# Moving a layer's input loads from ScalarE's queue to SyncE's, behind a small store

## The chip, the cores and the metric

The kernel runs on one core of one Trainium2 chip. The core has five engines that run their own instruction streams side by side: TensorE (PE in the profile; its weight loads are shown as PEld), VectorE (DVE), ScalarE (ACT), GpSimd (POOL) and SyncE (SP). A load or store is a DMA: one engine issues it, and the transfer then runs beside the engines. The issues of an engine stand in its program like its other instructions and are taken in order; the profile shows them as ACTq or SPq.

The metric is the time of one execution in microseconds (us), as the median of several runs.

## The reference

Four layers run one after the other on x, which is 4 sequences of 1024 tokens with 256 channels:

```python
x = x + _L0_attn_a_ref(_layernorm(x), W_in, b_in, params_log, W_mid, ...)   # linear recurrence
x = x + _L0_ffn_ref(_layernorm(x), ...)                                     # top-32 gated product
x = x + _L0_attn_b_ref(_layernorm(x), Wq, Wkv_down, Wk_up, Wv_up, Wo)       # attention, 8 heads
x = x + _L0_ffn_ref(_layernorm(x), ...)                                     # the same ffn again
```

The change lies in the first layer. Cut to what matters, it is:

```python
u = jnp.einsum('btd,edh->ebth', x, W_in) + b_in          # three products: in_r, in_i, o
lam = jnp.exp(jax.lax.complex(-nu, theta))
uc = jax.lax.complex(gamma * in_r, gamma * in_i)
_, h = jax.lax.associative_scan(combine, (f, uc), axis=1)   # h[t] = lam * h[t-1] + uc[t]
out2 = jnp.einsum('ebtd,edh->ebth', jnp.stack([h.real, h.imag]), W_mid) + b_mid
out = out2[0] - out2[1] + o
y = jax.nn.gelu(out @ w1_w + w1_b, approximate=False)
y = y @ w2_w + w2_b + out
y = (y - mean) * rsqrt(var + LN_EPS) * ln_g + ln_b
```

## The kernel before

The 4096 tokens are eight blocks of 512 (`NBLK` is 8). A block holds every second token of one sequence, so two blocks make a sequence, and the recurrence runs over pairs of tokens. Each block of x is a tile of 128 partitions by 4 by 256 values, 512 KB, and stays in on-chip memory through all four layers. `load_x(engine, blk)` (L1040) loads one block on the queue of the engine that is named.

The first layer is class `Lru`:

- Its constructor issues the weights' loads on ScalarE (L217, L223, L225) and splits the input weights into two parts each (L219 on ScalarE, L220 on POOL).
- `head(xs)` (L357) normalizes one block. VectorE takes statistics of four tiles (L133, L134) and forms the reciprocal roots in a chain of small steps (L55 to L66, L136). ScalarE applies them (L145), PE transposes (L147), and the transposed block is split into a cast (L160, ScalarE) and a difference (L161, VectorE), called xnt. The first such cast is remembered as `xnt_first`.
- `tables` and `first_weights` (L230, L277) make tables of cosines and sines (L269 to L275) and turned weights (L354, L355) on VectorE and ScalarE.
- `states(xnts, c)` (L381) makes the products into the "pu" banks (L170), evacuates them on ScalarE (L390) and runs the recurrence on VectorE (L402 to L416; L410 is the scan). Each evacuation is appended to `evacuated`; one call appends two.
- `outputs` (L422) makes, for one block, the products into the "po" banks (L170 and L437), evacuates them on ScalarE into ot (L438), multiplies by w1 (L443, "pu" banks), applies the gelu (L446), multiplies by w2 (L452, "po" banks again), adds on VectorE (L455), transposes back (L465), and normalizes; POOL multiplies by the gain and adds the base of `brow` (L482, L483) and adds the result to x (L484).

There are two banks each of "pu", "po", "py" and "pt". A block's outputs use the two "po" banks twice, and L455 is what frees them the second time.

`ffn_weights` (L984) loads and prepares what the second layer needs: `lint` (four loads, L1010), `wf` (L1011), and three rows, which go through a buffer `v` of one copy. For each row POOL clears v (L1017), three loads of 1 KB fill three of its partitions (L1019), and ScalarE and POOL turn it into a sum of three bf16 parts (L1020 to L1025; the results are linb twice and bias). The next row cannot be loaded before the last step on the one before is done.

The order in which each engine takes its instructions is fixed when the program is built: a scheduler simulates the program in time (`schedule_with_timeline_sim=True`, L1303), fills each engine with what is ready, and prefers what stands earlier in the text. `tc.issue_after(ins)` puts what the block under it holds behind `ins` in the order of one engine, the engine of `ins`; it is an order, not a wait for `ins` to end, and work that the block holds on other engines is not bound by it.

In the kernel before the loads stand as follows: blocks 0 and 1 on SP at the very start; the weights on ScalarE; blocks 2 and 3 on ScalarE behind `xnt_first`; `brow` on ScalarE behind the fourth evacuation; blocks 4 to 7 and all of `ffn_weights` on ScalarE behind the eighth evacuation, which is the last one of the second sequence.

Of the kernel before, what the change touches and what calls it, by code (L numbers as in the profile page):

```python
# [10 lines left out]
F32 = mybir.dt.float32  # L11
# [10 lines left out]
P = 128  # L22
B = 4
T = 1024
D = 256
# [3 lines left out]
NBLK = B * T // 512  # L29
# [143 lines left out]
def by_block(v):  # L173

    return [
        v[b * T : (b + 1) * T, :].rearrange("(q p r) d -> r p q d", p=P, r=CH)[r] for b in range(B) for r in range(CH)
    ]
# [796 lines left out]
def run(*gens):  # L974
    for g in gens:
        for _ in g:
            pass
# [6 lines left out]
def ffn_weights(nc, rp, cp, w, lint, lin_t, w_ffn, rows):  # L984
    vecs = w.vecs


    grp = cp.tile([P, 32], F32, tag="grp", name="grp")
    nc.gpsimd.memset(grp, 1.0)
    nc.gpsimd.affine_select(  # L990
        out=grp, in_=grp, compare_op=ALU.is_ge, fill=0.0, base=0, pattern=[[-4, 32]], channel_multiplier=1
    )
    nc.gpsimd.affine_select(
        out=grp, in_=grp, compare_op=ALU.is_ge, fill=0.0, base=3, pattern=[[4, 32]], channel_multiplier=-1
    )
    for s in range(2):
        for k in range(KD):
            nc.gpsimd.tensor_scalar(
                w.cw[:, k, s * 32 : (s + 1) * 32],
                grp,  # L1000
                vecs[:, V_CW + 2 * s + k : V_CW + 2 * s + k + 1],
                0.0,
                ALU.mult,
                ALU.add,
            )
    nc.gpsimd.memset(lint, 0.0)
    for s in range(2):
        for k in range(KD):
            r = k * 64 + s * 32
            nc.scalar.dma_start(lint[r : r + 32, s, :], lin_t[s, k * 32 : (k + 1) * 32, :])  # L1010
    nc.scalar.dma_start(w.wf, w_ffn)  # L1011

    nc.gpsimd.memset(w.ones, 1.0)
    parts = [slice(32 * i, 32 * i + 32) for i in range(3)]
    for dst, at in ((w.linb[:, 0:D], 0), (w.linb[:, D : 2 * D], D), (w.bias, 4 * D)):
        v = rp.tile([P, D], F32, tag="v", name="v")
        nc.gpsimd.memset(v, 0.0)  # L1017
        for i in range(3):
            nc.scalar.dma_start(v[32 * i : 32 * i + 1, :], rows[0:1, at : at + D])  # L1019
        nc.scalar.copy(dst, v)  # L1020
        nc.gpsimd.tensor_tensor(v, v, dst, ALU.subtract)
        for i in (1, 2):
            nc.scalar.copy(dst[parts[i], :], v[parts[i], :])
        nc.gpsimd.tensor_tensor(v[parts[2], :], v[parts[2], :], dst[parts[2], :], ALU.subtract)
        nc.scalar.copy(dst[parts[2], :], v[parts[2], :])  # L1025
# [3 lines left out]
def tile_kernel(ctx: ExitStack, tc: tile.TileContext, x_in, w_lru, vecs_in, rows, w_ffn, lin_t, w_attn, w_down, out):  # L1029
    nc = tc.nc  # L1030
# [9 lines left out]
    def load_x(engine, blk):  # L1040
        engine.dma_start(blocks[blk], by_block(x_in)[blk])
# [9 lines left out]
    w = Weights()  # L1051
    w.ident, w.vecs = ident, vecs
    w.wf = cp.tile([P, KD, D], F32, tag="wf", name="wf")
    lint = cp.tile([P, 2, D], F32, tag="lint", name="lint")
# [5 lines left out]
    f1 = Ffn("f1", tc, bp, x, w)  # L1060
# [3 lines left out]
    with ExitStack() as c1:  # L1064
        psum = Banks(c1.enter_context(tc.tile_pool(name="ps1", space=PSUM)), {"pu": 2, "po": 2, "py": 2, "pt": 2})

        brow = c1.enter_context(tc.tile_pool(name="brow", bufs=1)).tile([P, 2, D], F32, tag="brow", name="brow")
        lru = Lru(tc, c1, ident, vecs, brow, w_lru, psum)
        xb = [x[4 * k : 4 * k + 4] for k in range(NBLK)]
        xnt = [lru.head(xb[0])]  # L1070
        lru.tables(lambda: xnt.append(lru.head(xb[1])))
        with tc.issue_after(lru.xnt_first):
            for blk in range(2, 4):
                load_x(nc.scalar, blk)
        h = [[lru.states(xnt, c) for c in range(KD)]]
        lru.output_weights()
        with tc.issue_after(lru.evacuated[3]):
            nc.scalar.dma_start(brow.rearrange("p a b -> p (a b)"), rows[0, 2 * D : 4 * D].partition_broadcast(P))
        xnt += [lru.head(xb[k]) for k in (2, 3)]
        h.append([lru.states(xnt[2:4], c) for c in range(KD)])  # L1080
        for k in range(NBLK):
            last = k >= NBLK - 2
            if k == 0:
                with tc.issue_after(lru.evacuated[7]):
                    for blk in range(4, NBLK):
                        load_x(nc.scalar, blk)
                    ffn_weights(
                        nc, c1.enter_context(tc.tile_pool(name="rows", bufs=1)), cp, w, lint, lin_t, w_ffn, rows
                    )
            if k < NBLK - 1:  # L1090
                run(lru.outputs(k % CH, xb[k], xnt[k], h[k // CH], (0, 1), last))

            b = k // CH + 1
            if 2 <= b < B:
                if k % CH == 0:
                    h.append([])
                h[b].append(lru.states(xnt[b * CH : (b + 1) * CH], k % CH))
            if k + 4 < NBLK:
                xnt.append(lru.head(xb[k + 4]))
            if 2 <= k < NBLK - 2:  # L1100
                run(f1.head(k - 2, lru.sp, psum, "pt"))
        for blk in range(4, NBLK - 3):
            run(f1.head(blk, lru.sp, psum, "pt"))
        k = NBLK - 1
        ot, zt = lru.buffers()
        halves = [
            lru.outputs(k % CH, xb[k], xnt[k], h[k // CH], (i,), last, tag, [v[:, :, c : c + 256] for v in (ot, zt)])
            for i, tag, c in ((0, "pu", 0), (1, "po", 256))
        ]
        for i in (0, 0, 1):  # L1110
            next(halves[i])
        run(f1.head(NBLK - 3, lru.sp, psum, "pt"))
        for i in (0, 1, 0, 1, 0, 1, 1):
            next(halves[i])
        with tc.issue_after(lru.last_gelu):
            run(f1.head(NBLK - 2, lru.sp, psum, "pt"))
        run(*(f1.head(NBLK - 1, lru.sp, psum, "pu", (i,), "lx", "zt") for i in range(2)))

    with ExitStack() as c2:
# [7 lines left out]
        at = Attention(tc, x, ident, ident64, wqk, wvo, wd, sp, wp)  # L1127
        with ExitStack() as c4:
# [14 lines left out]
            first = at.prepare(0, 0, psum, "at")  # L1143
# [163 lines left out]
```

## Time and profile before

| what | us |
|---|---|
| median of three runs | 1532.92 |
| lowest and highest run | 1526.67, 1534.85 |
| the profiled execution | 1534.08 |
| its span, first to last instruction | 1532.4 |
| busy PE, DVE, ACT, POOL in the span | 1295.5, 1183.2, 1017.3, 681.6 |
| mean granted PE clock | 0.937 |
| issue of blocks 2 and 3 on ACTq | 15.79 and 16.23 |
| issue of brow on ACTq | 46.01 |
| issue of blocks 4 to 7 on ACTq | from 73.17 |
| first store of the first layer on SPq (L527) | 135.45 |

The first layer lasts until about 295 us, when SP begins to load for the second. A row of the timeline reads: start, length, engine, line, operation, output from inputs, shapes, how many; in brackets how long the engine had stood idle just before and what ended that. A row of the waits reads: who waited for whom, the total, how often, the longest. A row of the windows gives each engine's busy time in that stretch with the number of its instructions, then the clock that PE was granted (1.00 is full), the share of the DMA engines' time, and GB/s.

### The profile page before, as it was taken

To read this page: it belongs to the slowest core of one execution; us is meant where nothing else is said; L and a number is where in the kernel's file an instruction comes from. 1 tells how busy PE (TensorE), PEld (TensorE's weight loads), DVE (VectorE), ACT (ScalarE), POOL (GpSimd) and SP (SyncE) were. 2 spreads that over 40 slices of the span, in tenths; PEclk is the share of its full clock that TensorE was granted. 3 is DMA by queue.
4 is the path that set the end of the run, shared out by engine and by line. 5 is a ranking of instruction groups with operands and counts; after the bars stand their busy time and mean duration, and the time that the engine had idled before them with its cause. 6 is when DMAs were issued, how large, how long until landed. Compare 5 with 4: busy or idle time off the path is not lost. (4 is left out here: it accounts for less than half of the span.)

```text
span 1532.4 us, 28699 instructions
## 1 busy us (share of the span) xinstructions
PE 1295.5 (85%) x10136; PEld 960.3 (63%) x10136; DVE 1183.2 (77%) x3674; ACT 1017.3 (66%) x2148; POOL 681.6 (44%) x849
## 2 busy tenths in 40 slices
PE   5879998697898898888988989899999998666775
PEld 3635455376676766766766767677777776434454
DVE  8976665697878887878778687776676675499998
ACT  5353433466887877797778687877776776476664
POOL 2033332162545454544544543445443534067876
PEclk9989999699999999999999999999999999679888
DMA  3010000321454334434433335334445454000000
GB/s 117 26 47 15 19 23 21 123 94 56 76 98 89 64 76 74 73 74 80 84 73 69 68 72 87 62 71 84 70 75 92 73 95 83 1 15 24 22 25 28
DMA packets 288609, 96.51 MB, mean 63 GB/s; under 512 B 268233, under 2 KB 284626, under 8 KB 288466
## 3 DMA queue, kind: packets, MB, share of 16 engines
q1 hardware_dynamic: 283024, 88.50, 28.5%
q10 hardware_dynamic: 5442, 6.18, 1.2%
q8 instruction: 80, 1.31, 0.3%
q14 instruction: 63, 0.52, 0.1%
HBM read 16.01 MB, written 11.53 MB: 18 GB/s over the span
## 5 line engine op out<-in xcount | busy, mean ns | idle before, releaser
L893 POOL TENSOR_TENSOR pd<-pr,pd 128x1024 f16<-128x1024 f32 x128 | 273.3, 2141 | 247.5 <-ACT pd L892 183.2
L885 DVE TENSOR_REDUCE nm<-sc 128x1 f32<-128x1024 f32 x256 | 308.5, 1218 | 78.3 <-PE sc L881 76.9
L889 ACT ACTIVATE pr<-sc,nm 128x1024 f32<-128x1024 f32 x256 | 286.2, 1120 | 84.4 <-DVE nm L887 44.6
L881 PE MATMUL sc<-kh,qs 128*128 128x512 f32 x512 | 185.4, 440 | 26.3 <-ACT pr L889 18.7
L881 PE MATMUL sc<-kl,qs 128*128 128x512 f32 x512 | 163.2, 399 | 0.0
L905 ACT COPY p<-ptp 128x512 f32<-128x512 f32 x224 | 124.1, 591 | 47.6 <-PE ptp L900 39.5
L674 DVE MATCH_REPLACE8 wk<-m,wk 128x256 f32<-128x256 f32 x384 | 154.8, 406 | 0.1
L900 PE MATMUL ptp<-ident,pr 128*128 128x128 f32 x1024 | 140.1, 277 | 16.2 <-ACT pr L889 15.3
L674 DVE MAX8 m<-wk 128x8 f32<-128x256 f32 x384 | 150.2, 412 | 0.4
L925 PE MATMUL pmo<-p,la 128*64 128x128 f32 x2048 | 142.7, 287 | 5.5 <-ACT ft L524 2.9
L900 PEld LDWEIGHTS ptp<-ident,pr 128*128 128x128 f32 x1024 | 117.0, 141 | 39.2 <-ACT pr L889 25.9
L892 ACT CAST pd<-pr 128x1024 f16<-128x1024 f32 x128 | 133.4, 1056 | 5.8 <-DMA d<-pd 4.8
L925 PEld LDWEIGHTS pmo<-p,la 128*64 128x64 f32 x2048 | 121.8, 143 | 24.6 <-ACT ft L524 5.1
L881 PEld LDWEIGHTS sc<-kh,qs 128*128 128x128 f32 x512 | 85.8, 196 | 50.9 <-ACT pr L889 29.9
L881 PEld LDWEIGHTS sc<-kl,qs 128*128 128x128 f32 x512 | 97.7, 191 | 23.5 <-issue 1.4
L925 PE MATMUL pmo<-d,lb 128*64 128x128 f16 x3072 | 102.6, 222 | 8.0 <-DVE qs L853 2.6
L925 PEld LDWEIGHTS <-lb 128*64 128x64 f16 x3072 | 91.8, 111 | 25.8 <-issue 20.1
L628 POOL TENSOR_TENSOR ex<-ex,wk 128x512 f32<-128x512 f32 x61 | 77.7, 1273 | 58.5 <-DVE wk L674 50.6
L921 POOL COPY rows<-rs 128x128 f32<-128x128 f32 x128 | 36.1, 294 | 127.3 <-PE pmo L933 71.5
L936 DVE TENSOR_TENSOR on<-pmo,rb 128x128 f32<-128x128 f32 x128 | 36.5, 285 | 67.8 <-ACT rb L935 67.4
L699 PE MATMUL pf<-wf,vt 128*128 128x256 f32 x288 | 81.6, 424 | 4.1 <-ACT vt L697 3.4
L147 PE MATMUL pt<-ident,xn 128*128 128x128 f32 x256 | 47.7, 308 | 42.9 <-ACT xn L145 31.4
(306 smaller groups left out, 2779.6 us busy)
## 6 DMA issues: line engine op xcount, KB each, us to landing
tt<-ft SPq DMA_DIRECT2D x16, 256.0 KB
tt<-tt SPq DMA_DIRECT2D x8, 512.0 KB
out<-x SPq DMA_DIRECT2D x32, 128.0 KB
x<-in_x ACTq DMA_DIRECT2D x6, 512.0 KB
pf<-pfs SPq DMA_DIRECT2D x12, 256.0 KB
full<-pf SPq DMA_DIRECT2D x24, 128.0 KB
d<-pd SPq DMA_TRANSPOSE x128
wa<-in_w_attn SPq DMA_DIRECT2D x2, 640.0 KB
```

The costliest lines, as they stand in the source:

```text
L147: nc.tensor.transpose(pt[:, k, i * P : (i + 1) * P], xn[:, k * P : (k + 1) * P], ident)
L628: pool.tensor_tensor(ex, ex, wk, ALU.subtract)
L674: ins = make(*args).ins
L699: nc.tensor.matmul(dst, vt[:, k, :], w.wf[:, k, :], start=(k == 0 and bias is None), stop=(k == KD - 1))
L881: nc.tensor.matmul(sc[:, sl], qs[:, j, q * P : (q + 1) * P], kk[:, sl], start=(i == 0), stop=(i == 1))
L885: nc.vector.tensor_reduce(nm, sc, AX.X, ALU.max, negate=True)
L889: nc.scalar.activation(pr, sc, AF.Exp, bias=nm, accum_out=ssum[:, j : j + 1])
L892: nc.scalar.copy(pd[:, 0, :], pr)
L893: nc.gpsimd.tensor_tensor(pd[:, 1, :], pr, pd[:, 0, :], ALU.subtract)
L900: nc.tensor.transpose(pt[:, kk, :], pr[:, kc * P : (kc + 1) * P], self.ident)
L905: nc.scalar.copy(dst, pt)
L925: nc.tensor.matmul(po[j * HD : (j + 1) * HD, 0, :], v, pts[j][:, c, :], start=(n == 0), stop=(n == len(terms) - 1),)
```

## The change

All loads that ScalarE issued after the weights leave its queue, except blocks 2 and 3, which now follow directly behind the weights without an order of their own. SP issues a store of one column of the first normalized block (128 partitions by 4 bytes) to a new DRAM tile `gate`; it needs the first cast of xnt. `brow`, blocks 4 to 7 and the loads in `ffn_weights` are issued by SP behind that store. The store's instruction is also what `ffn_weights` stands behind, where it was the eighth evacuation, an instruction of ScalarE.

```diff
@@ ffn_weights
-            nc.scalar.dma_start(lint[r : r + 32, s, :], lin_t[s, k * 32 : (k + 1) * 32, :])
-    nc.scalar.dma_start(w.wf, w_ffn)
+            nc.sync.dma_start(lint[r : r + 32, s, :], lin_t[s, k * 32 : (k + 1) * 32, :])
+    nc.sync.dma_start(w.wf, w_ffn)
...
-            nc.scalar.dma_start(v[32 * i : 32 * i + 1, :], rows[0:1, at : at + D])
+            nc.sync.dma_start(v[32 * i : 32 * i + 1, :], rows[0:1, at : at + D])
@@ tile_kernel
         lru = Lru(tc, c1, ident, vecs, brow, w_lru, psum)
+        for blk in range(2, 4):
+            load_x(nc.scalar, blk)
         xb = [x[4 * k : 4 * k + 4] for k in range(NBLK)]
         xnt = [lru.head(xb[0])]
         lru.tables(lambda: xnt.append(lru.head(xb[1])))
-        with tc.issue_after(lru.xnt_first):
-            for blk in range(2, 4):
-                load_x(nc.scalar, blk)
+
+        gate = f1.dram.tile([P, 1], F32, tag="gate", name="gate")
+        first = nc.sync.dma_start(gate, xnt[0][0][:, 0, 0:1].bitcast(F32)).ins
+        with tc.issue_after(first):
+            nc.sync.dma_start(brow.rearrange("p a b -> p (a b)"), rows[0, 2 * D : 4 * D].partition_broadcast(P))
+            for blk in range(4, NBLK):
+                load_x(nc.sync, blk)
         h = [[lru.states(xnt, c) for c in range(KD)]]
         lru.output_weights()
-        with tc.issue_after(lru.evacuated[3]):
-            nc.scalar.dma_start(brow.rearrange("p a b -> p (a b)"), rows[0, 2 * D : 4 * D].partition_broadcast(P))
...
-                with tc.issue_after(lru.evacuated[7]):
-                    for blk in range(4, NBLK):
-                        load_x(nc.scalar, blk)
+                with tc.issue_after(first):
                     ffn_weights(
```

## The prediction

> **What bounds the kernel now.** I read the page's 40 slices first, then the ScalarE timeline around the moved loads, the waits there, the busy time by stretch, and the VectorE timeline. Times in us.
>
> The slices (38.3 each) show the place: in the first three PE reads 5, 8, 7 before its run of 9s, while DVE reads 8, 9, 7. Most of the moved loads are issued at 73, at the end of the second.
>
> ```profile
> PE   5879998697898898888988989899999998666775
> DVE  8976665697878887878778687776676675499998
> ACT  5353433466887877797778687877776776476664
> ```
>
> ScalarE's own timeline there (ACTq is its queue of issues):
>
> ```profile
> 73.16 0.78 ACT L390 ACTIVATE u<-pu,gb,par_o 128x512 f32<-128x512 f32 x1 [2.01 <-DVE h L402]
> 73.17 2.05 ACTq L1041 DMA_DIRECT2D x<-in_x  x4
> 75.25 2.10 ACTq L1010 DMA_DIRECT2D lint<-in_lin_t  x4
> 77.40 0.43 ACTq L1011 DMA_DIRECT2D wf<-in_w_ffn  x1
> 78.58 4.34 ACTq L1019 DMA_DIRECT2D v<-in_rows  x3
> 82.97 1.26 ACT L438 ACTIVATE ot<-po,ob 128x512 f32<-128x512 f32 x2 [9.03 <-DMA lint<-in_lin_t]
> ```
>
> Twelve loads stand in ScalarE's program ahead of the first evacuation of L438. The last three issues take 4.34, while the same three take 0.84 at 88.16 and again at 95.35: they wait for the block loads to land (the DMA rate falls from 337 GB/s in 80 to 82 to 39 in 82 to 84). The waits from 74 to 95 (total, times, longest) name who pays:
>
> ```profile
> ACT ot L438 <- DMA lint<-in_lin_t: 9.0, 1, 9.0
> ...
> PE pz L443 <- ACT ot L438: 8.0, 1, 8.0
> ...
> DVE ot L455 <- issue: 2.2, 1, 2.2
> ```
>
> So PE stands for 8.0 and then runs at a granted clock of 0.50 (78 to 88): its eight L443 matmuls take 5.82 where L452's eight take 3.70. That looks like 8.0 + 2.1 = 10.1 to win. But VectorE's column (third pair: busy, then count) says otherwise:
>
> ```profile
> core 0: us, PE busy (x) PEld busy (x) DVE busy (x) ACT busy (x) POOL busy (x), PEclk, DMA share, GB/s
> ...
> 62.00:76.00 14.00, 13.70 (x46) 8.21 (x44) 12.89 (x20) 2.34 (x3) 0.00 (x0) 1.00 0.12 38
> 76.00:84.00 8.00, 0.30 (x1) 0.30 (x2) 7.93 (x20) 1.03 (x2) 0.00 (x0) 0.61 0.75 246
> 84.00:92.00 8.00, 6.46 (x10) 2.42 (x10) 7.77 (x47) 4.80 (x10) 1.93 (x3) 0.75 0.01 2
> 92.00:94.00 2.00, 2.00 (x6) 0.95 (x5) 0.00 (x0) 1.67 (x4) 0.82 (x2) 1.00 0.03 8
> ```
>
> VectorE is full through PE's gap: 56.74 of 57 from 5 to 62, then 12.89 of 14, 7.93 of 8, 7.77 of 8. Its first real gap is the 2.21 before L455:
>
> ```profile
> 85.69 0.65 DVE L415 TENSOR_TENSOR h<-h,u 128x512 f32<-128x512 f32 x1
> ...
> 91.44 0.36 DVE L134 BATCH_NORM_AGGREGATE lx_mv<-lx_st 128x2 f32<-128x6 f32 x4
> 94.01 0.75 DVE L455 SCALAR_TENSOR_TENSOR ot<-pz,vecs,ot 128x512 f32<-128x512 f32 x1 [2.21 <-issue]
> ```
>
> L455 adds the result of block 0 and frees the two "po" banks that block 1's outputs need. PE cannot go far past it, and VectorE reaches it at 91.8 at the earliest in its present order. **Two chains meet at L455**: ScalarE and PE at 94.0, VectorE at 91.8.
>
> **The change, part by part.**
>
> **ScalarE's issues leave.** 19 go to SP: four blocks 2.05, four lint 2.10, wf 0.43, nine rows 4.34 + 0.84 + 0.84, brow 0.35. What ends is the 9.03 wait at L438 and two later stops of 1.28 and 0.60, before the table load at 89.03 and the cast at 96.23, each after a row load that had waited for a cleared buffer. Without them the ScalarE and PE chain would reach L455 about 10 earlier, at 84. On its own VectorE's order allows 91.8, so the term is **-2.2**. If the order lets L455 overtake the statistics of blocks 5 to 7 it is more. From 76.6 to 91.8 VectorE spends 15.2, of which the six 0.58 steps, two 1.12 scans of the states take 5.7, so 9.5 belongs to the four blocks' heads, 2.4 a block; only block 4 is needed at once, so the bound is 91.8 - 7.1 = 84.7, or -9.3. I take -2.2: in the present order all 16 statistics (L133, 76.7 to 91.5) stand ahead of L455, and their data will only come sooner.
>
> The Trainium skill, "DMA: Bandwidth & Descriptors", section "Rules for kernel authors", speaks against the change: spreading DMAs over the issuing engines gives no bandwidth and saves sequencer issue time alone. By that rule ScalarE would gain only the unhindered issues, 2.05 + 2.10 + 0.43 + 0.84 = 5.4, and be free at 78.6. The trace shows 4.4 more, the waits for landing in the same stop. The sum is the same by both, since VectorE decides.
>
> **SP takes them behind a gate.** The gate is one store of 128 x 4 bytes that waits for the first cast of xnt (15.92 to 16.48); an issue costs 0.23 to 0.53 by the rows above. Behind it queue brow, blocks 4 to 7, lint, wf and the rows; behind those the first store of L527 at 135.45. SP issues nothing from 1.8 until then, so its waits for landing or for a cleared v cost 0; without that cover the same 9.03 would hold the L527 stores. Some 2.25 MB at the 372 GB/s of 18 to 20 take 6.1, so block 7 lands near 25 instead of 82, and the rows a little later. First users are VectorE's statistics at 76.67 and POOL's L482 at 106.44: 0, covered by 50 and more. Lower bound 0, since nobody waited for them to land but ScalarE's issues.
>
> **Blocks 2 and 3 move from 15.79 and 16.23 to about 5.4.** Two issues (0.40 + 0.52) fit in ScalarE's 4.53 wait before its first cast at 7.34: 0, or at most 0.5 if the second waits for block 1 to land (its statistics begin at 6.84). Their 1.05 MB follow the weights (366 GB/s until 12.0, then 21) and land near 15 instead of 20. VectorE waited only 0.12 at 18.99 to 19.23 for them, so the gain is at most 0.1. If they mixed with the weights, w_o and the rest would land up to 2.8 later; w_o's first use in a product is L320 at 32.1. I take 0.
>
> **Blocks 4 to 7 are there early.** What VectorE does for them (up to 9.5) can be put between 34, when block 2's mean slot is free (L136 at 34.03), and 62. There VectorE has no gap, so the states move back as much as the statistics move forward. Up to L455 the amount is conserved: 0. Two items can now slip in front of L455: block 4's two xnt differences (L161, 2 x 0.69, in the present run at 96.85 and 103.42), **+1.4**, and block 6's chain, which in the present run stands at 97.46 to 101.46 and 109.95 to 116.9 for two blocks; bounds 0 and +1.4.
>
> **What gets lighter behind L455.** Block 4's eight transposes (0.60 + 0.38 + 0.38 among PE's full 16.00 of 94 to 110) go into PE's gap: **-1.4**. At 114.6 PE waits 3.04 for the second L455, which stands behind such a lx chain stretched to 0.65 a step; bounds 0 and -3.0, and I take half, **-1.5**.
>
> **The casts of linb and bias are no longer held.** `issue_after` orders only work of the named instruction's engine; that was ScalarE, now it is SP. So L1020, L1023 and L1025 may come anywhere after their rows land. Each set costs ScalarE 0.40 + 0.81 + 0.40 and two waits for POOL of 1.06 and 0.84, 3.5; three sets 10.5. From 20 to 50 ScalarE is busy 20.32 of 30, so 9.7 is free. Bounds 0 and +10.5; I take **0**, as ScalarE's idle time there is nearest to the need.
>
> **Sum:** -2.2 + 1.4 - 1.4 - 1.5 = -3.7. The profiled execution took 1534.08 (span 1532.4 and 1.7 around it), so 1530.4; it lies 1.2 above the median of 1532.92. I predict 1530. The rest of the kernel just starts earlier: PE is busy 7 to 10 of every 10 from 94 to 230.
>
> **Rivals.**
>
> **The whole stall comes back.** L455 overtakes the later statistics: -9.3 - 1.4 = 1523.4. For it: PE's wait and slow clock are plain, and from 94 on PE is the full engine. Against it: VectorE's column, full from 5 to 91.8.
>
> **The freed casts hold ScalarE in the opening.** They stand in its program between 25 and 50, and its queue is in order, so xnt casts, evacuations (L390) and table steps (L272) wait with them, and VectorE with those. Price +10.5 less the 2.2 of slack at L455: 1542.4, slower. Against it: 9.7 of idle ScalarE time. It decides from the point where VectorE's idle time before 62, now 0.3, passes 2.2; to be told from no change it needs 9.9.
>
> **The new order itself.** The engines' orders are made at build time by a simulation (L1303), so later stages may be ordered otherwise; no row prices this. The nearest are two stops of PE, 3.0 for L455 at 114.6 and 4.2 for L66 (line of norm_f, in the waits from 94 to 300): their sum either way, 7.2, and I allow 10 on the bad side since a stop is followed by slow matmuls as at 84.
>
> **How the numbers follow.** Forecast 0.45 (1526 to 1536), whole stall 0.23, freed casts 0.22, new order 0.10. I call 0.5%, 7.7, what a measurement can tell from no change, so faster means below 1525.3 and slower above 1540.6. Faster: 0.04 of the forecast's, 0.18, 0, 0.03, together 0.25. Slower: 0.02, 0, 0.13, 0.05, together 0.20. Same: 0.55. For 8 in 10 the range reaches past both rivals' middles: 1518 to 1545; the forecast's own is 1526 to 1536.
>
> **What would show it.** Right: no issue of a load on ACTq after 7; PE's 8.0 wait at L443 gone and its clock not at 0.50 there; L455 between 90 and 94, with VectorE full until then. Whole stall: L455 at 84 to 86, with statistics after it. Freed casts: linb and bias casts before 50 with VectorE idle over 2.2 beside them. Wrong altogether if VectorE had gaps before 62 that early data fills, or if the change of time arises after 300.

## The result, and the profile after

| | before | after |
|---|---|---|
| median of seven runs each | 1530.52 | 1540.33 |
| lowest and highest run | 1524.83, 1534.85 | 1534.19, 1545.92 |
| the profiled execution, its span | 1534.08, 1532.4 | 1545.92, 1544.2 |
| mean granted PE clock in it | 0.937 | 0.925 |
| first L455 on VectorE | 94.01 | 100.64 |
| first product of the second layer (L556, PE) | 300.10 | 303.60 |

The ratio of after to before is 1.0056, with a 95% interval of 1.0034 to 1.0078: the change made the kernel slower, by 9.8 us in the medians (8.6 by the ratio), against a forecast of 3.7 faster. One run of the variant e5 below, 2134.34 at a granted clock of 0.587, is slow and is left out of every figure. The profiled execution of after is the slowest of its seven runs, so its 11.8 over the profiled one of before is not the size of the effect.

ScalarE was relieved as forecast. The last load that its queue issues stands at 8.06 (block 3), and the waits of 8.0 and 9.0 at L443 and L438 are gone. A stop appeared on VectorE instead, some fifty microseconds earlier in the kernel. SyncE's timeline of after:

```profile
16.50 0.34 SPq L1076 DMA_DIRECT2D gate<-xnt  x1
16.90 0.42 SPq L1078 DMA_DIRECT2D brow<-in_rows  x1
17.37 9.66 SPq L1041 DMA_DIRECT2D x<-in_x  x4
27.13 3.49 SPq L1010 DMA_DIRECT2D lint<-in_lin_t  x4
30.72 0.36 SPq L1011 DMA_DIRECT2D wf<-in_w_ffn  x1
```

The four block loads took 9.66 to issue where they had taken 2.05 on ScalarE's queue. VectorE's timeline of after, just behind, shows the statistics of block 4 standing in front of the tables:

```profile
23.25 0.17 DVE L134 BATCH_NORM_AGGREGATE lx_mv<-lx_st 128x2 f32<-128x6 f32 x1
30.80 0.75 DVE L133 BATCH_NORM_STATS2 lx_st<-x 128x6 f32<-128x256 f32 x2 [7.38 <-DMA x<-in_x]
31.47 0.16 DVE L120 TENSOR_SCALAR cs_c<-cs_t 128x20 f32<-128x20 f32 x1
...
100.64 0.75 DVE L455 SCALAR_TENSOR_TENSOR ot<-pz,vecs,ot 128x512 f32<-128x512 f32 x1
```

VectorE, which the forecast had taken as full until 62, stood 7.38 for a block that had not landed. L455 came 6.6 later than before. The waits of after from 0 to 110 pass it on (5.0 of the first row's 12.4 is the wait for block 0, which every version has):

```profile
DVE lx_st L133 <- DMA x<-in_x: 12.4, 2, 7.4
ACT t L272 <- DVE lx_rs L66: 10.8, 1, 10.8
PEld pw L290 <- DVE tw L355: 10.6, 4, 7.7
...
ACT linb L1020 <- DMA v<-in_rows: 2.2, 1, 2.2
```

The stretches of after (PE, PEld, DVE, ACT and POOL busy, then the clock, the DMA share and GB/s):

```profile
5.00:62.00 57.00, 33.38 (x128) 23.85 (x129) 48.15 (x249) 31.06 (x72) 10.38 (x23) 0.88 0.40 112
62.00:76.00 14.00, 8.24 (x27) 5.80 (x26) 14.00 (x31) 4.70 (x8) 0.00 (x0) 0.76 0.00 0
76.00:84.00 8.00, 8.00 (x31) 5.27 (x30) 8.00 (x22) 2.24 (x4) 0.00 (x0) 1.00 0.00 1
```

From 5 to 62 VectorE lost 8.6 of busy time against before (48.15 against 56.74). PE no longer stands in 76 to 84 (8.00 against 0.30), but now stands in 62 to 76 (8.24 against 13.70, at a clock of 0.76); its longest wait there, 3.63, is for VectorE's L161. The hole moved from behind the states to ahead of them.

Why had block 4 not landed? The DMA rows tell it: first after, while the DMA works on what stands behind the gate, then before, while the same brow travels alone:

```profile
DMA packets 235, 0.18 MB, mean 16 GB/s; under 512 B 146, under 2 KB 153, under 8 KB 235
```

```profile
DMA packets 144, 0.26 MB, mean 37 GB/s; under 512 B 16, under 2 KB 16, under 8 KB 144
```

In after it is the stretch from 16 to 27, in before 45 to 52, where all of brow's 0.26 MB passed in some 2 us. In after 0.18 MB took eleven. In the records of the packets, brow's 128 pieces of 2048 B each took a mean of 0.54 us (the longest 1.78, from 19.9 to 28.9) against 0.118 before (the longest 0.438). What stood directly ahead of them was the gate: 128 pieces of 4 B, each written to DRAM. The gate store itself was slow to complete: its completion signals come from 19.87 to 24.20, up to 7.7 after its issue at 16.50 (in e1 below, where it goes to on-chip memory, from 18.24 to 18.44, 1.8 after its issue).

### The profile page after: what moved, and what is told of

Its sections match the earlier page's. It is cut to its first block, busy times and chain, and to the rows that moved or that the text cites. A ratio compares the mean times of both kernels' runs of the same rounds, so it can differ in the third digit from the quotient of the medians.

```text
span 1544.2 us, 28700 instructions
## 1 busy us (share of the span) xinstructions
PE 1310.3 (85%) x10134; PEld 971.9 (63%) x10136; DVE 1175.1 (76%) x3674; ACT 1016.2 (66%) x2148; POOL 680.8 (44%) x849
## 5 line engine op out<-in xcount | busy, mean ns | idle before, releaser
L925 PE MATMUL pmo<-p,la 128*64 128x128 f32 x2048 | 146.5, 291 | 6.2 <-ACT ft L524 2.9
L556 PE MATMUL pl<-lint,xc_f 128*128 128x512 f32 x128 | 77.5, 694 | 10.2 <-ACT xc_f L587 10.2
```

Source lines behind the costliest of these rows:

```text
L556: self.last_logits = nc.tensor.matmul(v, x, w.lint, start=False, stop=True).ins
L925: nc.tensor.matmul(po[j * HD : (j + 1) * HD, 0, :], v, pts[j][:, c, :], start=(n == 0), stop=(n == len(terms) - 1),)
```

## The experiments

In the table, "L556" is the first product of the second layer and stands for the end of layer one. "Behind" is the difference of the medians less that of L556: what the three later layers gave back. L455 and L556 come from one profile for each kernel, the medians from runs beside the kernel before on the same chip. The clock is the mean over the runs.

| kernel | L455 | L556 to before | median, before | ratio (95%) | behind | clock |
|---|---|---|---|---|---|---|
| before | 94.01 | 0 (300.10) | | | | 0.9427 |
| after | 100.64 | +3.5 | 1540.33, 1530.52 | 1.0056 (1.0034 to 1.0078) | +6.3 | 0.9320 |
| e1 gate on chip | 93.55 | -6.3 | 1532.31, 1530.73 | 1.0001 (0.9984 to 1.0018) | +7.9 | 0.9355 |
| e2 brow last | 99.07 | +1.1 | 1537.21, 1530.73 | 1.0045 (1.0025 to 1.0065) | +5.4 | 0.9319 |
| e3 casts held | 100.2 | 0.0 | 1540.92, 1530.73 | 1.0063 (1.0046 to 1.0081) | +10.2 | 0.9382 |
| e4 late on SP | 84.22 | -14.8 | 1531.92, 1530.73 | 0.9998 (0.9978 to 1.0018) | +16.0 | 0.9381 |
| e5 gate as a row | 93.05 | -4.1 | 1531.49, 1529.98 | 1.0008 (0.9992 to 1.0024) | +5.6 | 0.9336 |
| e6 gate of 32 | 97.37 | -2.3 | 1535.17, 1529.98 | 1.0038 (1.0024 to 1.0052) | +7.5 | 0.9329 |
| e7 late on ScalarE | 94.07 | -2.7 | 1536.51, 1529.98 | 1.0041 (1.0027 to 1.0056) | +9.2 | 0.9392 |
| e8 statistics held | 96.70 | +2.3 | 1542.63, 1529.98 | 1.0083 (1.0061 to 1.0105) | +10.4 | 0.9338 |
| e9 later as before | 85.35 | -11.1 | 1523.32, 1532.11 | 0.9952 (0.9937 to 0.9966) | +2.3 | 0.9407 |
| e10 later as after | 83.00 | -9.7 | 1525.97, 1532.11 | 0.9962 (0.9950 to 0.9974) | +3.6 | 0.9380 |
| e11 late on SP, sixth | 85.60 | -14.2 | 1523.14, 1532.11 | 0.9951 (0.9932 to 0.9969) | +5.2 | 0.9420 |

### What the gate does: e1, e5, e6, e2

All four keep the orders of PE, VectorE, ScalarE and GpSimd exactly as in after. In e1, e5 and e6 only the gate differs, so nothing but the transfers can make the difference.

e1 puts the gate's 128 pieces of 4 B into on-chip memory:

```diff
-        gate = f1.dram.tile([P, 1], F32, tag="gate", name="gate")
+        gate = cp.tile([P, 1], F32, tag="gate", name="gate")
```

> The gate's 128 x 4 bytes go to on-chip memory instead of DRAM; every engine's order stays that of the changed kernel. Theory (the 4-byte writes to DRAM make the brow load behind them take 10 us instead of 2, so block 4 lands at 30.8 and VectorE stands 7.4): brow lands by 20, VectorE's stop before block 4's statistics falls from 7.4 to under 1, the second evacuation-and-add (first L455) comes at 93 to 95 instead of 100.6, and the median falls by 3 to 8 against the changed kernel, to 1532 to 1537. Rival (brow is slow by itself early, or on SP's queue): stop still 6 to 8, median 1538 to 1543. Rival (the stop does not matter, the new order of later stages does): stop gone, median within 2 of 1540.

e5 writes the same 512 bytes to DRAM from one partition, as one row:

```diff
-        gate = f1.dram.tile([P, 1], F32, tag="gate", name="gate")
-        first = nc.sync.dma_start(gate, xnt[0][0][:, 0, 0:1].bitcast(F32)).ins
+        gate = f1.dram.tile([1, P], F32, tag="gate", name="gate")
+        first = nc.sync.dma_start(gate, xnt[0][0][0:1, 0, 0:P].bitcast(F32)).ins
```

> The gate store goes to DRAM as before the experiment, but as one row of 512 bytes from one partition instead of 128 pieces of 4 bytes; same bytes, same queue, same orders as the changed kernel. Theory (many 4-byte pieces into the same few DRAM lines slow the load behind them): brow's packets of 2 KB back to about 0.1 to 0.2 us each, VectorE's stop under 1, median 1530 to 1535 as with the on-chip gate. Rival (any DRAM write of SP's queue ahead of the loads does it): stop 6 to 8, median 1538 to 1543.

e6 writes 32 pieces of 4 B to DRAM (`[32, 1]`, from partitions 0 to 31):

> The gate store has 32 pieces of 4 bytes instead of 128, all else as in the changed kernel, orders the same. If the delay grows with the number of pieces (10 us for 128): brow lands after some 2 to 4.5 us, VectorE's stop 0 to 2, median 1531 to 1537. If one piece or any such store costs the whole delay: stop 6 to 8, median 1538 to 1543.

SyncE's timeline of e1:

```profile
16.68 0.55 SPq L1076 DMA_DIRECT2D gate<-xnt  x1
17.28 0.58 SPq L1078 DMA_DIRECT2D brow<-in_rows  x1
17.91 2.23 SPq L1041 DMA_DIRECT2D x<-in_x  x4
```

VectorE's L455 in e1, and its stretch from 5 to 62:

```profile
93.55 0.77 DVE L455 SCALAR_TENSOR_TENSOR ot<-pz,vecs,ot 128x512 f32<-128x512 f32 x1
```

```profile
5.00:62.00 57.00, 34.85 (x138) 24.59 (x138) 54.94 (x261) 33.89 (x77) 10.52 (x22) 0.93 0.35 112
```

The transfers from 16 to 27, in e1 and then in e6:

```profile
DMA packets 2422, 2.39 MB, mean 217 GB/s; under 512 B 231, under 2 KB 2279, under 8 KB 2422
```

```profile
DMA packets 944, 1.02 MB, mean 93 GB/s; under 512 B 78, under 2 KB 816, under 8 KB 944
```

Thirteen times as much as in after passes behind the gate on chip, and block 4 is there in time, if only just (it lands at 23.47 in e1, and its first statistics begin at 23.56): VectorE has no stop for a block in e1 or in e5 (54.94 busy of 57 in e1), the block loads are issued in 2.2 in both, and L455 stands at 93.55 and 93.05. With 32 pieces to DRAM the harm is about half: VectorE's timeline of e6 has

```profile
27.67 0.75 DVE L133 BATCH_NORM_STATS2 lx_st<-x 128x6 f32<-128x256 f32 x2 [4.15 <-DMA x<-in_x]
```

and L455 lies between. Both ranges expected of e6 for the stop (0 to 2, and 6 to 8) missed the 4.15: a quarter of the pieces does half the harm. So it is the number of small pieces written to DRAM, neither the bytes (e5 writes the same 512), nor DRAM as such, nor the number of pieces as such (e1 writes as many). Step for step it goes into the median: after, e6, e5 and e1 stand 9.8, 5.2, 1.5 and 1.6 over before. The 128 pieces cost 8.2 of the 9.8; by the ratios it is 8.4, with some 4 either way from the two intervals. All pieces go to neighbouring places in DRAM, 512 bytes in all; whether pieces far apart do the same was not tried.

e2 asks whether brow, which is loaded into every partition from one row, is itself what is slow. It is issued behind the four blocks:

```diff
-            nc.sync.dma_start(brow.rearrange("p a b -> p (a b)"), rows[0, 2 * D : 4 * D].partition_broadcast(P))
             for blk in range(4, NBLK):
                 load_x(nc.sync, blk)
+            nc.sync.dma_start(brow.rearrange("p a b -> p (a b)"), rows[0, 2 * D : 4 * D].partition_broadcast(P))
```

> brow is queued behind blocks 4 to 7 on SP; the orders of the other engines stay those of the changed kernel. If the DRAM gate store slows whatever load comes next, block 4's load is slow instead of brow's: it lands at 27 or later and VectorE still stands 4 to 8. If brow's own 128-fold read of one row is slow, block 4 lands near 21, the stop is under 1, the first L455 comes at 93 to 95, and the median is 1532 to 1537. If only the new order of later stages matters: stop gone and median within 2 of 1540.

VectorE's timeline of e2:

```profile
28.40 0.75 DVE L133 BATCH_NORM_STATS2 lx_st<-x 128x6 f32<-128x256 f32 x2 [5.07 <-DMA x<-in_x]
```

Now it is the blocks' own pieces that crawl: from 18 to 26 between 2 and 70 of them start in a microsecond, and one took 4.8. Whatever comes next behind the gate is slow. Brow is not the cause; it only stood there, and without it ahead 2.3 of the stop are saved.

The Trainium skill, "DMA: Bandwidth & Descriptors", section "Why small descriptors are slow (HBM only)", says that small pieces are expensive on the DRAM side and not between on-chip memories. The runs agree on which side it is: 8.2 between DRAM and on chip. In them the cost fell on the loads queued behind the small pieces, 16 GB/s in after against 217 in e1 over the same stretch.

### Whether the freed casts matter: e3, e8

```diff
-                with tc.issue_after(first):
+                with tc.issue_after(first), tc.issue_after(lru.evacuated[7]):
                     ffn_weights(
```

> The casts of linb and bias on ScalarE stand behind the eighth evacuation again, as before the change; all else as changed. Rival of the prediction (the freed casts hold ScalarE in the opening): ScalarE's 2.2 wait for v before 37 and VectorE's 1.0 beside it vanish, first L455 moves up by over 5, median 1530 to 1535. Theory (block 4's late load): VectorE's stop of 7.4 stays, first L455 by 0 to 2 earlier, median within 4 of 1540.

With the casts behind the eighth evacuation again, as before, VectorE's stop remains, in e3's timeline and waits:

```profile
29.93 0.75 DVE L133 BATCH_NORM_STATS2 lx_st<-x 128x6 f32<-128x256 f32 x2 [6.57 <-DMA x<-in_x]
```

```profile
DVE lx_st L133 <- DMA x<-in_x: 11.6, 2, 6.6
ACT t L272 <- DVE lx_rs L66: 10.0, 1, 10.0
```

L455 stands at 100.2, 0.4 earlier than in after. The freed casts were not what made the changed kernel slower: the ratio is no better (1.0063). They may not be free for the rest of layer one, which ends 3.5 earlier than in after, by one profile of each.

e8 leaves the DRAM gate and the freed casts, and puts the heads of blocks 4 to 7 on VectorE behind the first sequence's second recurrence, so that none of them can stand in the opening:

```diff
-                xnt.append(lru.head(xb[k + 4]))
+                with tc.issue_after(lru.scanned[1]):
+                    xnt.append(lru.head(xb[k + 4]))
```

> The changed kernel with its DRAM gate, but VectorE's work on blocks 4 and later stands behind the end of the first sequence's recurrence, so a late block 4 meets no VectorE waiting in order. Theory (the loss in the first layer is VectorE standing in its order for block 4): brow still takes 10 us and block 4 still lands near 30, VectorE has no stop over 1 for it, first L455 at 84 to 95 instead of 100.6, first layer ends 5 to 12 earlier than with the change. Rival (the late data itself costs, whoever waits): first L455 at 98 or later. The median is open, since the later layers are ordered anew: 1525 to 1540.

VectorE's stop for block 4 is gone, and ScalarE stands instead. ScalarE's timeline of e8:

```profile
37.45 0.40 ACT L1020 CAST linb<-v 128x256 bf16<-128x256 f32 x1 [11.10 <-DMA v<-in_rows]
```

A cast of linb stands in ScalarE's order at 26, for a row that the slow gate lets land at 37. The waits of e8 up to 60 show PE standing 11.6 for the cast of f (L160) behind it:

```profile
POOL v L1021 <- ACT linb L1020: 15.7, 2, 12.5
PEld pu L170 <- ACT f L160: 11.8, 1, 11.8
PE pu L170 <- ACT f L160: 11.6, 1, 11.6
```

VectorE in turn stands 10.22 for a ScalarE step (L354) behind that cast. So layer one ends only 1.2 earlier than in after, where 5 to 12 was expected, L455 misses its 84 to 95, and the median lies above its 1525 to 1540. The freed casts can thus hold ScalarE for as long as the rival put it (10.5), but by a wait for a late row, not by the casts' own time as the rival had added it up. In e1, with the same freed casts, the wait is 2.5, and VectorE stands 1.39 at 30.37 for a ScalarE step behind it. That nothing but the gate makes the rows late here was not tried with e8's order.

### What the relief of ScalarE is worth: e4, e7, e11

e4 is the kernel before with blocks 4 to 7 and ffn_weights' loads on SyncE, at their old time: behind a small copy on ScalarE and an on-chip gate.

```diff
...
+                mark = cp.tile([P, 2], F32, tag="mark", name="mark")
                 with tc.issue_after(lru.evacuated[7]):
+                    nc.scalar.copy(mark[:, 0:1], vecs[:, 0:1])
+                first = nc.sync.dma_start(mark[:, 1:2], mark[:, 0:1]).ins
+                with tc.issue_after(first), tc.issue_after(lru.evacuated[7]):
                     for blk in range(4, NBLK):
-                        load_x(nc.scalar, blk)
+                        load_x(nc.sync, blk)
...
```

> The kernel before, with only the late loads (blocks 4 to 7, lint, wf, the rows) on SP at their old time, behind a small copy on ScalarE and a 4-byte on-chip transfer; blocks 2, 3 and brow as before, casts held as before. It leaves ScalarE's 9.0 stop out and nothing else. Forecast of the prediction (VectorE decides at L455): L455 at 91 to 93 instead of 94.0, median 1525 to 1531 against 1530.5 for before. Rival (the whole stall comes back): L455 at 84 to 87, median 1519 to 1524.

VectorE's timeline of e4:

```profile
84.22 0.73 DVE L455 SCALAR_TENSOR_TENSOR ot<-pz,vecs,ot 128x512 f32<-128x512 f32 x1
```

L455 comes 9.8 earlier, where the prediction's rival of the whole stall put it (84 to 86) and not where the forecast did (91 to 93): in e4's order 24 statistics (L133) stand ahead of it on VectorE, in before 32. Layer one ends 14.8 earlier. Yet the median is that of before (0.9998), where the rival expected 1519 to 1524: the later layers give 16.0 back. e7 is the control. It adds the same copy and gate, but leaves all loads on ScalarE's queue, so that the first layer stays what it was (99.5% of VectorE's instructions in the same sequence), while the later layers are ordered anew (70%):

> A control: the kernel before with only a small copy on ScalarE and one 4-byte on-chip transfer added behind the eighth evacuation; all loads stay on ScalarE, ScalarE's 9 us stop stays, the first layer's order stays nearly that of before (DVE 0.995 alike), but the scheduler orders the later layers otherwise (DVE 0.70 alike). Theory (the order that a new schedule gives the later layers is worth several us by itself, here a loss as in e4): first layer ends within 1.5 of before, and the median differs by 3 to 12, upward. Rival (later orders are all worth the same): median within 2 of 1530.7.

Its L455 stands at 94.07, and it is 6.5 slower than before (1.0041). Its layer one ends 2.7 earlier, where 1.5 either way was expected. So a new plan of the layers that the edit does not touch can cost that much. The new order is what is known to differ there; whether the added tile also moved others in memory was not looked at.

e11 is e4 with the copy behind the sixth evacuation in place of the eighth, which happens to leave the later order nearer to that of before (VectorE 91% in place of 80%):

> The kernel before with blocks 4 to 7 and ffn_weights' loads on SyncE, behind a small copy of ScalarE that stands behind the sixth evacuation in place of the eighth, and an on-chip gate of 4 bytes a partition; ffn_weights' own work stays behind the eighth evacuation. The later order is nearer to the kernel before than in the run with the eighth (VectorE 91% in place of 80%, GpSimd 97% in place of 88%). Theory: the first layer ends 12 to 16 earlier, as there; the later cost falls from the 16 there to between 3 and 10, and the median is 1520 to 1527. Rival (what the first layer gains beyond some 6 is given back whatever the order): 1530 to 1533, as there.

Layer one ends 14.2 earlier, 5.2 are given back, and 1523.14 is left, 9.0 under before (0.9951, 0.9932 to 0.9969). Both numbers of the theory hold.

### Where the later layers lose: e9, e10

Both have the gate on chip, the casts behind the eighth evacuation as in e3, and the heads of blocks 4 to 7 held as in e8: in e9 behind scanned[1], in e10 behind scanned[2]. That one index decides the order of the later layers: in e9 it is nearly the one of before, in e10 the one of after.

> The changed kernel with the gate in on-chip memory, the heads of blocks 4 to 7 on VectorE behind the first sequence's second recurrence (scanned[1]), and ffn_weights' own work on ScalarE behind the eighth evacuation. The engines' orders of the first layer differ from both kernels; those of the layers behind it are nearly the order of the kernel before (98% of VectorE's, over 99% of the other engines' instructions in the same sequence). Theory (the later layers' order costs the changed kernel and its five relatives some 6.5, whatever the first layer does): with the order of before that cost is gone, so the median stands against the kernel before as the end of the first layer does, within 3; with no stop of VectorE in the opening and no 9.0 stop of ScalarE the first layer ends 4 to 9 earlier, the median 1522 to 1528. Rival (the later layers give back what the first one gains, in whatever order): the median within 2 of before or above it, 1529 to 1533. Rival (the late cost is the new DMA queueing or the place of tiles in memory, not the order): some 6.5 behind the first layer's gain here as well.

> As the run with the later order of the kernel before, but the heads of blocks 4 to 7 stand behind the second sequence's first recurrence (scanned[2]) in place of the first sequence's second. That alone makes the later layers' order the one of the changed kernel (over 99.9% in the same sequence). Theory: whatever the end of the first layer is against the kernel before, the median is 6.5 (4 to 9) above that difference. Rival (the later order does not matter): the median stands to the end of the first layer as in the run with the order of before, within 2.

e9 is 8.8 faster than before, with layer one 11.1 earlier (4 to 9 was expected), and in its stretch from 62 to 76 PE no longer stands:

```profile
62.00:76.00 14.00, 14.00 (x53) 9.76 (x52) 14.00 (x49) 4.53 (x7) 0.00 (x0) 1.00 0.00 1
```

So what layer one gains is not always given back, and the rival that said so falls. But e10 lost only 3.6 behind layer one, not 4 to 9, and stands 1.3 from e9 in what it gave back, inside the 2 of the rival that said that the later order does not matter. So the pair does not show that after's later order costs 6.5. The explanation from the order alone fails here, and with e3 too, whose later order is 95% that of before and which still gave back 10.2.

The column of clocks goes further. Among the runs of one kernel the time goes with the clock: over the 171 runs with a clock on record 0.01 less goes with 7.0 us more (slope -697, from a fit within the kernels). Put every kernel at before's clock of 0.9427 by that slope, and the kernels with after's later order (after, e1, e2, e5, e6, e10) have -1.2, +2.9, -2.1, -0.8, +0.7 and +0.3 left behind layer one: all within 3, which is as much as one profile can tell (the control's layer one is off by 2.7). Their loss goes with lower clocks. Whether the clock is the cause, or only a trace of PE's stops, this does not say, and a part of after's lower clock lies in layer one already (0.88 from 5 to 62, 0.94 before). For e3, e4, e7, e8 and e11 it leaves 4 to 13 (e9 0.9), so there something beside the clock lost time; their later order is the one thing in those layers that their edits are known to have changed. The clock in 40 equal slices (in tenths of full) shows one place where it fell, on the pages of before and of e1:

```profile
PEclk9989999699999999999999999999999999679888
```

```profile
PEclk9999999697799999999999999999999999778888
```

In e1 two slices from 344 to 421 read 7 where before has 9s. After has 8s there, and e5, with e1's order, an 8 and a 9. So the order alone does not fix it. What the lower clocks come from was not settled.

The Trainium skill, "TensorE: Matmul & The Clock Gate", section "What's actually happening", says that the gate follows how busy TensorE has lately been, by a window that runs free of the kernel. The stretches from 62 to 76 agree with the first in the rough only (14.00 busy of 14 at 1.00 in e9, 8.24 at 0.76 in after, but 10.52 at 0.63 in e6), and the spread of one kernel's clocks from run to run (0.925 to 0.940 in after's seven) would follow from the second, which no run here shows.

## Why the prediction was wrong

**The step that failed** is "SP takes them behind a gate", with its price of 0: "Some 2.25 MB at 372 GB/s take 6.1, so block 7 lands near 25", "covered by 50 and more", "Lower bound 0, since nobody waited for them to land". Two things were wrong in it. The rate was taken from block loads with nothing in front of them; behind 128 pieces of 4 B into DRAM it was 16 GB/s until 27, and block 4's statistics could begin only at 30.8. And the cover was read from the old order (statistics at 76.67), although a later step of the same text said that VectorE's work for these blocks would move to between 34 and 62. It moved to 23.4, in front of the data. Even with the gate on chip nothing was left of the cover: in e1 block 4 lands 0.1 before VectorE asks for it. The price was +7.4 at VectorE, +7.1 at L455 (100.64 against e1's 93.55) and 8.2 of the median (9.8 less e1's 1.6, some 4 either way).

**"Up to L455 the amount is conserved: 0"** holds where the data is there (e1 and e5) and not where the order asks for it too early.

**The two chains at L455** were read rightly. With a harmless gate the change's own order puts L455 at 93.55 and 93.05; -2.2 and +1.4 from 94.0 make 93.2. The mechanism fits too: in both VectorE stands nowhere between 48.6 and L455, and 13 of the xnt differences (L161) stand ahead of it, in before 11, which are the two that the prediction let slip in front. The sum of the first layer, -3.7, measured -6.3 and -4.1 at L556. The gain stays small because VectorE is full, as the text said; where another order lets L455 pass other VectorE work (e4, e9 to e11), it comes at 83.0 to 85.6, so the bound of -9.3 (84.7) was real, and e10's 83.0 lies below it.

**The freed casts at 0** hold in the changed kernel up to L455: e3 moves it by 0.4. As a mechanism they exist, as e8 shows, and at a small price in e1 (VectorE's 1.39). Blocks 2 and 3 were issued at 7.34 and 8.06, not at about 5.4 as put; no wait for them appeared, so the 0 stands.

**"The rest of the kernel just starts earlier"** failed as well, in the way that the prediction had named as a sign of being wrong altogether: of the 9.8, 3.5 stand at the end of layer one and 6.3 arise behind it. All eleven variants and the changed kernel gave back between 2.3 and 16.0 behind layer one. Some 2 to 3 of that may lie in the one profile of before, since the control, with a nearly unchanged first layer, also ends it 2.7 earlier. The rival of the new order was allowed 7.2 either way, 10 on the bad side, and a chance of 0.10; a control that does nothing else cost 6.5. With the gate mended (e1) the change would have been no change: 1.0001. One small slip of the sum: 1534.08 less 3.7 is 1530.4, but as that profiled execution lies 1.2 above the median, the forecast for the median is 1529.2, and the freed casts' 1542.4 is 1541.2. Nothing hangs on it.

So the slower outcome has two parts by the runs: the gate, 8.2, shown by kernels with the same orders of PE, VectorE, ScalarE and GpSimd; and what layer one's relief should have brought and the later layers took back, in e1 7.9, of which 5.0 go with a lower clock of PE, and whose cause stays open.

## What to carry to other kernels

A tiny store that only marks a time is not free for the queue behind it: give it one row or an on-chip target. A load moved earlier invites a scheduler to put its users earlier still, so price it by the first use in the new order, and by what stands ahead of it in the queue. And where a scheduler plans the whole program, an edit in one layer re-plans all of them: measure a control with the same edit and no effect, and look for the variant that keeps both the gain and a good later order, such as e9 (1523.32) or e11 (1523.14), which beat both kernels.

## What the runs showed of the hardware that was not expected

- 128 stores of 4 B to DRAM slowed the loads queued behind them to 16 GB/s over 11 us; 32 such stores to 93, one store of 512 B or 128 of 4 B on chip not at all (217 in e1). The packets' own time in the records, 9 ns each, does not show it; the gate store's completion does, up to 7.7 after its issue against 1.8 on chip.
- An issue can last long while the loads ahead of it crawl: of the 9.66 that SyncE's four block loads took to issue, the third one alone took 7.88 (18.39 to 26.27); in e1 all four took 2.23. The row loads' 4.34 on ScalarE's queue in before was something else: three issues of 0.47, 0.23 and 0.23, each begun 0.02 to 0.03 after blocks 4, 5 and 6 had landed in turn (78.56, 80.92, 82.67), where without such waits the three took 0.84.
- Runs of one kernel differ by up to 15 us (e2: 1532.9 to 1548.0, clocks 0.938 to 0.922), and the time goes with the mean granted clock, 7.0 us for 0.01.
